# A sum placed between two sets of subtractions, and the last stores with their queues exchanged

## The chip, the cores and the metric

The kernel runs on one core of a Trainium2 chip. The metric is the device time of one execution in microseconds (us); lower is better. Engines are named as in the profile: PE is TensorE (matmuls), DVE is VectorE, ACT is ScalarE, POOL is GpSimd, SP is SyncE, which issues DMAs here and computes nothing. "ACTq" and "SPq" are the DMA-issuing sides of ScalarE and SyncE.

## The reference

A cross-conditioned mixture of three experts over B = 8 batches of T = 512 tokens with H = 256 features, all in float32:

```python
nx = layer_norm(x)                                   # (8, 512, 256)
weights = softmax(nx @ Wq @ (ctx @ Wk)^T / 16)       # 64 context rows per batch
evidence = weights @ (ctx @ Wv)
combined = concat([nx, evidence, anchor])            # 768 features
probs = softmax(combined @ router_W + router_b)      # 3 experts
h = silu(combined @ e_w1 + e_b1)                     # (8, 512, 3, 512)
routed = sum over experts of probs * (h @ e_w2 + e_b2)
g = sigmoid(silu(combined @ gate_w1 + gate_b1) @ gate_w2 + gate_b2)
return x + g * (routed @ out_w + out_b)
```

## The kernel before

The work is a loop of four passes (`j` from 0 to 3), each over two batches, called rows 0 and 1. Before the loop weights are loaded, products of weights are formed (`e_w2 @ out_w`, for instance, becomes `w2o`), and the first two batches are normalized. A pass runs `gate_layer`, three times `expert_layer`, and `outputs`. Everything is kept transposed: features on the 128 partitions, the 512 tokens along the free axis. A float32 product of 128x128 weights with 512 columns shows in the profile as two MATMUL rows of PE.

The products of 2x2 blocks (two feature halves by two batches) are computed with seven block products in place of eight, in the manner of Strassen and Winograd: sums and differences of weight blocks are prepared once (`w2s`, picked by `combo(S1)`, `combo(S2)`, `combo(S4)`), and differences of the hidden tiles are formed by VectorE in `subtract` (line 1072), which overwrites one block of the hidden tiles with the difference of two. One call of `subtract` issues three instructions, one for each expert, each over 128x1024 elements. `experts(ps, lhs, k, i)` issues the six products (twelve MATMUL rows, line 796) that contract one block of hidden tiles, over all experts, into one bank of TensorE's accumulators. The banks are called `u`, `z` and `y` in `outputs`. A bank goes on accumulating from one block product to the next: the intermediate value is added to a result tile (`r11`, `r12`, `r21`, `r22`) by VectorE and the next products are added on top. That sum is `keep` (line 1088), one VectorE instruction over 128x512 elements which reads the bank and adds it to the result tile.

So around the change the order in `outputs` is: products into `u`, `keep(r11, u)`, products into `z`, two calls of `subtract`, `keep(r22, z)`, products into `u` with `combo(S2)`, `keep(r12, u)`. The second products into `u` read the block that the first `subtract` writes. The block that the second `subtract` writes is read two or more product groups later. In passes 0 to 2 there follow products into `y` and again into `u`, with parts of the next pass between them (`run(...)`), before `z` is used again with `combo(S4)`. In the last pass `z` is used right after.

The program order on each engine is the order in which the code issues its instructions (`manual_schedule`); waits between engines are set from the tiles that they share. Each engine works its instructions off in that order, so an instruction that waits holds up those behind it.

At the end of the last pass things differ from the other passes. Row 0's lower half of features is finished token by token: the tokens are taken as the partition axis, in four tiles of 128 tokens (`token_experts`, six products of 128x128 for each tile, into banks 2, 0, 5 and 3). `turn_rest` transposes the gate and the partial result on TensorE and ScalarE copies them into `rest`. `finish_late` finishes row 0's upper half and stores it as four pieces of `hg`, two on ScalarE's queue and two on SyncE's. Then `finish_rows` (lines 1177 to 1180) runs for each of the four token tiles: a product and a sum on VectorE, and one store of 64 KB from `y_rows`. The stores of tiles 0 and 2 go to SyncE's queue and those of tiles 1 and 3 to ScalarE's. A DMA issue on any of these queues also waits until an earlier DMA that has the same completion semaphore has landed; eight such semaphores are used in turn by the DMAs of both queues.

Of the kernel before, what the change touches and what calls it, by code (L numbers as in the profile page):

```python
# [16 lines left out]
def kernel(  # L17
# [51 lines left out]
    nc = tc.nc  # L69
# [28 lines left out]
    def bank(i, name):  # L98
        return psum.tile([P, 512], F32, tag=f"b{i}", name=name)
# [908 lines left out]
    def outputs(j, steps):  # L1008
        last = j == NP - 1

        def run(point):
            for step in steps.get(point, ()):
                step()
# [17 lines left out]
        u, z, y = (bank(i, f"ps_g{n}_{j}") for n, i in (("u", 0), ("z", 2), ("y", 4)))  # L1031
# [25 lines left out]
        def experts(ps, lhs, k, i, start=False):  # L1057
            for q in range(NQ):
                product(ps, lhs(q), hidden(j, q, k, i), start=start and q == 0)

        def combo(s):
            return lambda q: w2s[:, s, q, :]

        def subtract(dst, other):

            (k, i), (k2, i2), (k3, i3) = dst, *other
            for e in range(E):
                d, p, m = (
                    S["h", ii, e].rearrange("p (q k) t -> p q k t", k=2)[:, :, kk, :]
                    for kk, ii in ((k, i), (k2, i2), (k3, i3))  # L1070
                )
                nc.vector.tensor_tensor(d, p, m, ALU.subtract)  # L1072

        def bias_sum(role, i, row):

            r = work.tile([P, T], F32, tag=role, name=f"{role}_{j}", bufs=1)
            nc.scalar.activation(
                by_side(r), pb[:, row, :, 1, :], AF.Identity, bias=b2o[:, i, 0:1],
                scale=b2o[:, i, 1:2],
            )  # L1080
            for e in range(2, E):
                nc.vector.scalar_tensor_tensor(  # L1082
                    by_side(r), pb[:, row, :, e, :], b2o[:, i, e : e + 1], by_side(r), ALU.mult, ALU.add
                )
            return r

        def keep(r, ps):
            nc.vector.tensor_tensor(r, r, ps, ALU.add)  # L1088
# [32 lines left out]
        def finish_late(r, ps, i, row):  # L1121
# [5 lines left out]
        r11, r22, r12, r21 = (  # L1127
            bias_sum(f"r{i + 1}{row + 1}", i, row) for i, row in ((0, 0), (1, 1), (0, 1), (1, 0))
        )
        ug = u  # L1130
        u, y, z = (bank(i, f"ps_{n}2_{j}") for i, n in ((1, "u"), (3, "y"), (5, "z")))
# [4 lines left out]
        run("P1")  # L1136
        experts(z, combo(S1), 0, 1, start=True)
        subtract((0, 1), ((1, 1), (0, 1)))
        subtract((0, 0), ((0, 1), (0, 0)))
        keep(r22, z)  # L1140
        run("P5")
        experts(u, combo(S2), 0, 1)
        keep(r12, u)
# [17 lines left out]
        def turn_rest(r):  # L1161

            rest = work.tile([P, 2, NT, P], F32, tag="xg", name="rest", bufs=1)
            for n, part in enumerate((S["hg", 0, 0], r)):
                pt = misc(f"pt_rest_{n}")
                for t in range(NT):
                    ts = slice(t * P, (t + 1) * P)
                    nc.tensor.transpose(pt[:, ts], part[:, ts], ident)
                nc.scalar.copy(rest[:, n, :, :].rearrange("p t c -> p (t c)"), pt)
            return rest  # L1170
# [6 lines left out]
        def finish_rows(y, rest, ps, t, queue):  # L1177
            nc.vector.tensor_tensor(y, ps, rest[:, 0, t, :], ALU.mult)
            nc.vector.tensor_tensor(y, y, rest[:, 1, t, :], ALU.add)
            queue.dma_start(out[2 * j, t * P : (t + 1) * P, :P], y)  # L1180
# [8 lines left out]
        rest = turn_rest(r11)  # L1189
        experts(u, lambda q: a(q, 1, 1), 0, 1)  # L1190
        tokens = [bank(b, f"ps_tokens_{b}")[:, :P] for b in (2, 0, 5, 3)]
# [2 lines left out]
        finish_late(r21, u, 1, 0)  # L1194
        y = work.tile([P, NT, P], F32, tag="yb", name="y_rows")
        for t in range(NT):
            finish_rows(y[:, t, :], rest, tokens[t], t, nc.scalar if t % 2 else nc.sync)


    with tc.manual_schedule(engines=None):  # L1200
# [62 lines left out]
        for j in range(NP):  # L1263
# [80 lines left out]
            for e in range(E):  # L1344
                expert_layer(j, e, within)
            outputs(j, between)


# [32 lines left out]
```

## Time and profile before

| | |
|---|---|
| median of 3 runs | 462.98 us (462.89 to 463.24) |
| profiled execution, device time | 463.12 us |
| its span (first to last event shown) | 461.3 us |
| mean granted TensorE clock | 0.999 |
| PE busy | 456.4 us (99%) |
| DVE busy | 365.2 us (79%) |
| ACT busy | 214.7 us (47%) |
| POOL busy | 100.4 us (22%) |

The span is what the profile covers; the execution's own time is 1.8 us longer and is what the runs are compared by. Times in the text are microseconds from the start of the span unless they are durations. In lists of instructions the first number is the start, the second the length, then engine, line, operation, output <- inputs, and in brackets how long the engine had been idle and what ended it. TensorE's matmuls overlap, so the length of a row is longer than the distance to the next one; distances between starts are the better measure.

### The profile page before, as it was taken

Reading aid. Unit: us, or ns where it says so; the run is one execution under the profiler, and the core shown is the slowest. Engines: PE = TensorE matmul, PEld = TensorE weight load, DVE = VectorE, ACT = ScalarE, POOL = GpSimd, SP = SyncE. Lnnn points to the kernel's source line nnn. Section 1 sums busy time; section 2 is a strip of 40 time slices with the busy share of each in tenths; the row PEclk is TensorE's granted clock in tenths of the full one; section 3 lists DMA queues with packets and bytes.
Section 4 is the critical chain, followed back from the end, with each engine's and each line's share of the span. In section 5 each row is a group of like instructions: output and inputs, shape, how many; then the busy total and the mean of one; then the engine's idle time right before and its main releaser. Section 6 shows DMA issues by size and latency. Waiting matters only on the chain.

```text
span 461.3 us, 4752 instructions
## 1 busy us (share of the span) xinstructions
PE 456.4 (99%) x1455; PEld 210.1 (46%) x1455; DVE 365.2 (79%) x683; ACT 214.7 (47%) x370; POOL 100.4 (22%) x149
## 2 busy tenths in 40 slices
PE   9999999999999999999999999999999999999996
PEld 7544555444444444444444444444444444444445
DVE  2988979969799669869799659879889625787973
ACT  3445683664222666556221576548221456457000
POOL 6357715001181200001072300001072300000020
PEclk9999999999999999999999999999999999999999
DMA  8975677302013326802012235702011570000013
GB/s 275 370 158 128 102 232 126 83 0 46 7 23 46 76 87 142 159 18 46 6 24 32 37 136 120 110 0 46 6 24 23 82 195 0 0 0 1 0 22 70
DMA packets 119401, 35.27 MB, mean 76 GB/s; under 512 B 106044, under 2 KB 116336, under 8 KB 118864
## 3 DMA queue, kind: packets, MB, share of 16 engines
q1 hardware_dynamic: 115312, 27.02, 28.9%
q0 software_dynamic: 2176, 7.17, 4.7%
q10 hardware_dynamic: 1888, 0.79, 0.6%
q8 instruction: 11, 0.18, 0.2%
q14 instruction: 14, 0.11, 0.1%
HBM read 27.56 MB, written 7.39 MB: 76 GB/s over the span
## 4 chain that ended last, share of the span: by engine, by line
PE 95%; DVE 4%; issue 0%
PE ps_u L796 43%; PE ps_z L796 18%; PE ps_y L796 14%; PE ps_vw L771 5%; PE ps_gu L796 3%; PE ps_w2o L501 2%; PE ps_s L649 2%; PE ps_gz L796 1%; DVE h L1072 1%; PE ps_tokens L796 1%; PE ps_wake L294 1%; DVE h L880 1%; PE ps_v L339 1%; PE ps_m L339 1%; PE ps_gy L796 1%; DVE r L1082 0%
## 5 line engine op out<-in xcount | busy, mean ns | idle before, releaser
L880 DVE TENSOR_TENSOR h<-h,pb 128x512 f32<-128x512 f32 x96 | 61.9, 694 | 6.5 <-ACT h L829 6.5
L796 PE MATMUL ps_u<-h,w2o 128*128 128x512 f32 x144 | 64.2, 595 | 0.0
L829 ACT ACTIVATE h<-h,abias 128x512 f32<-128x512 f32 x72 | 49.6, 719 | 13.5 <-DVE h L835 13.0
L796 PE MATMUL ps_u<-nxT,w 128*128 128x512 f32 x112 | 55.3, 604 | 0.0
L796 PE MATMUL ps_z<-wT,vw 64*128 64x512 f32 x104 | 49.5, 605 | 0.0
L1105 POOL TENSOR_TENSOR yb<-yb,xb 128x512 f32<-128x512 f32 x14 | 17.8, 1269 | 142.9 <-DVE yb L1104 138.8
L796 PE MATMUL ps_z<-h,w2s 128*128 128x512 f32 x96 | 42.6, 593 | 0.2 <-DVE r L1088 0.2
L796 PEld LDWEIGHTS ps_u<-h,w2o 128*128 128x128 f32 x144 | 27.0, 190 | 32.7 <-issue 29.4
L838 ACT COPY h<-ps_u 128x512 f32<-128x512 f32 x48 | 28.0, 582 | 29.4 <-PE ps_u L796 26.9
L415 POOL DMA_DIRECT2D vrd<-vw x8 | 5.0, 630 | 136.9 <-ACT vw L778 136.9
L1072 DVE TENSOR_TENSOR h<-h,h 128x1024 f32<-128x1024 f32 x24 | 34.3, 1483 | 0.0
L796 PEld LDWEIGHTS ps_u<-nxT,w 128*128 128x128 f32 x112 | 20.2, 189 | 29.5 <-issue 24.2
L829 ACT ACTIVATE h<-ps_u,abias 128x512 f32<-128x512 f32 x24 | 16.5, 688 | 29.7 <-PE ps_z L796 29.4
L796 PEld LDWEIGHTS ps_z<-h,w2s 128*128 128x128 f32 x96 | 18.1, 190 | 23.5 <-issue 21.8
L796 PE MATMUL ps_y<-nxT,w 128*128 128x512 f32 x56 | 28.6, 592 | 0.0
L796 PE MATMUL ps_z<-T,ws 128*128 128x512 f32 x56 | 28.6, 592 | 0.0
L835 DVE TENSOR_TENSOR h<-h,ps_y 128x512 f32<-128x512 f32 x24 | 16.4, 683 | 14.8 <-PE ps_y L796 14.0
L796 PE MATMUL ps_u<-wT,vw 64*128 64x512 f32 x56 | 27.8, 611 | 0.0
L796 PE MATMUL ps_y<-wT,vw 64*128 64x512 f32 x56 | 27.0, 596 | 0.0
L771 PE MATMUL ps_vw<-w,vT 128*128 128x512 f32 (+1 forms) x64 | 26.9, 542 | 0.0
L796 PE MATMUL ps_u<-T,ws 128*128 128x512 f32 x56 | 26.6, 592 | 0.0
L796 PE MATMUL ps_u<-T,w 128*128 128x512 f32 x56 | 26.6, 592 | 0.0
(229 smaller groups left out, 792.2 us busy)
## 6 DMA issues: line engine op xcount, KB each, us to landing
pb<-pd POOLq DMA_DIRECT2D x4, 1536.0 KB, 6.5
xb<-in_x_dram SPq DMA_DIRECT2D x64, 64.0 KB, 2.4
out_dram<-yb SPq DMA_DIRECT2D x56, 64.0 KB, 2.0
w<-in_L_xcond_e_w_dram SPq DMA_DIRECT2D x6, 512.0 KB, 10.1
x<-in_x_dram SPq DMA_DIRECT2D x24, 128.0 KB, 2.9
xd<-x SPq DMA_DIRECT2D x24, 128.0 KB, 2.4
xg<-xd SPq DMA_DIRECT2D x48, 64.0 KB, 2.4
scr_wa<-in_L_xcond_e_w_dram SPq DMA_DIRECT2D x3, 512.0 KB, 16.5
```

What stands on the lines that cost most here:

```text
L339: nc.tensor.matmul(ps, w_sb[:, k, m * P : (m + 1) * P], src[:, k, :], start=(k == 0), stop=(k == KH - 1))
L415: nc.gpsimd.dma_start(S["vrd", j][i].rearrange("e c -> c e"), S["vw", j][row_half(i), R0:])
L501: nc.tensor.matmul(ps[:, d * H : (d + 1) * H], w2T[:, k, (i + d) * P : (i + d + 1) * P], ow_sb[:, k, :], start=(k == 0), stop=(k == KH - 1),)
L649: nc.tensor.matmul(ps[side(i, h), g * NH : (g + 1) * NH], mr[:, k, 2 * j + i, g * TB : (g + 1) * TB], S["nxT", 2 * j + i][:, k, h * NH : ( ...
L771: nc.tensor.matmul(ps, vT[:, k, j * 2 * CT : (j + 1) * 2 * CT], w1[:, KH + k, n0:n1], start=(k == 0), stop=(k == KH - 1),)
L796: nc.tensor.matmul(ps, lhsT, rhs, start=start, stop=True, skip_group_check=not start)
L829: nc.scalar.activation(h, h if src is None else src, AF.Silu, bias=abias[:, c, 2 * j + i : 2 * j + i + 1])
L835: nc.vector.tensor_tensor(h, h, part, ALU.add)
L838: nc.scalar.copy(chunk(n, i, d), part)
L880: nc.vector.tensor_tensor(h, h, S["pb", j][:, i, :, 2 * q // RC, :], ALU.mult)
L1072: nc.vector.tensor_tensor(d, p, m, ALU.subtract)
L1105: nc.gpsimd.tensor_tensor(yb, yb, S["xb", 2 * j + row][:, i, :], ALU.add)
```

## The change

It has two parts. In `outputs`, in all four passes, VectorE's sum `keep(r22, z)` is issued between the two calls of `subtract` instead of after the second. In the last pass, the four stores of `y_rows` have their queues exchanged: tiles 0 and 2 are issued from ScalarE's queue and tiles 1 and 3 from SyncE's. No instruction is added or removed.

```diff
         run("P1")
         experts(z, combo(S1), 0, 1, start=True)
         subtract((0, 1), ((1, 1), (0, 1)))
+        keep(r22, z)
         subtract((0, 0), ((0, 1), (0, 0)))
-        keep(r22, z)
         run("P5")
         experts(u, combo(S2), 0, 1)
         keep(r12, u)
...
         finish_late(r21, u, 1, 0)
         y = work.tile([P, NT, P], F32, tag="yb", name="y_rows")
         for t in range(NT):
-            finish_rows(y[:, t, :], rest, tokens[t], t, nc.scalar if t % 2 else nc.sync)
+            finish_rows(y[:, t, :], rest, tokens[t], t, nc.sync if t % 2 else nc.scalar)
```

## The prediction

> **What bounds the kernel now.** I read the page first, for the span and for what each engine waits on; then the chain of waits over the last pass, because both edits can only count where that chain passes; then the timeline around the two places.
>
> The page:
>
> ```profile
> span 461.3 us, 4752 instructions
> PE 456.4 (99%) x1455; PEld 210.1 (46%) x1455; DVE 365.2 (79%) x683; ACT 214.7 (47%) x370; POOL 100.4 (22%) x149
> L796 PE MATMUL ps_z<-h,w2s 128*128 128x512 f32 x96 | 42.6, 593 | 0.2 <-DVE r L1088 0.2
> ```
>
> TensorE is busy 456.4 of 461.3 us, so only two things can shorten the run: fewer gaps between matmuls, or a shorter head or tail where no matmul runs. The third line shows a gap that belongs to the change: of the 96 matmuls into the bank `z` (four passes of 24), the whole group waited 0.2 us in the run, and VectorE's sums of L1088 (`keep`) ended that wait.
>
> The chain of waits, last pass (start, length, what):
>
> ```profile
> 427.43 0.60 DVE r L1088
> 428.03 6.81 DVE h L1072 x6
> 434.84 0.61 DVE r L1088
> 435.45 0.04 issue
> 435.49 5.42 PE ps_z L796 x12
> 440.91 5.15 PE ps_u L796 x12
> 446.06 0.87 PE pt_rest L1168 x8
> 446.93 5.32 PE ps_u L796 x12
> 452.25 5.37 PE ps_tokens L796 x48
> ```
>
> Up to 435.45 the end of the run hangs on VectorE: a sum, six subtractions, another sum. From 435.49 on it hangs on TensorE until the tokens. The DVE line at 434.84 is `keep(r22, z)`, the instruction that the change moves. The timeline there, with the two neighbouring matmul groups:
>
> ```profile
> 429.98 5.31 PE L796 MATMUL ps_u<-h,w2s 128*128 128x512 f32 x12
> 431.35 3.49 DVE L1072 TENSOR_TENSOR h<-h,h 128x1024 f32<-128x1024 f32 x3
> 434.76 0.68 DVE L1088 TENSOR_TENSOR r<-r,ps_z 128x512 f32<-128x512 f32 x1
> 435.36 0.68 DVE L1088 TENSOR_TENSOR r<-r,ps_u 128x512 f32<-128x512 f32 x1
> 435.49 5.42 PE L796 MATMUL ps_z<-h,w2s 128*128 128x512 f32 x12 [0.20 <-DVE r L1088]
> 440.75 5.31 PE L796 MATMUL ps_u<-h,w2o 128*128 128x512 f32 x12
> ```
>
> The group at 435.49 accumulates on into `z`, so it must not start before `keep(r22, z)` has read the bank. That read ends at 435.44.
>
> The tail: the timeline, then SyncE's own waits (line, what it waited for, us in total, times, longest), then the DMA issues (us from issue to landing last).
>
> ```profile
> 457.98 0.29 DVE L1179 TENSOR_TENSOR y_rows<-y_rows,rest 128x128 f32<-128x128 f32 x1
> 458.30 0.36 ACTq L1180 DMA_DIRECT2D out_dram<-y_rows  x1
> ```
>
> ```profile
> SPq L1376 <- DMA out_dram<-y_rows: 2.1, 1, 2.1
> SPq L1180 <- DMA out_dram<-hg: 1.6, 1, 1.6
> ```
>
> ```profile
> out_dram<-y_rows ACTq DMA_DIRECT2D x1, 64.0 KB, 1.7
> ```
>
> Tile 3's store leaves on ScalarE's queue 0.03 us after its sum, lands 1.7 us later at 460.0, and the end of the program follows at 461.3. Note the second wait: tile 0's store, on SyncE's queue, was ready at 455.03 but was issued at 456.99, because it first waited for an earlier `hg` store to land. With tile 0 that wait hides.
>
> **The change part by part.**
>
> *Sum moved ahead of the second subtractions, passes 1 to 3.* No instruction is added or removed; on VectorE one sum moves past three subtractions, in each of four passes. It can only hurt if `z` is not complete at the new place. In pass 2 the matmuls into `z` end at 219.23 and the new place is 220.75; in pass 4 it is 430.14 against 431.35. The margin is 1.2 to 1.5 us, and it is built in: the third subtraction of the first set overwrites tiles that the last matmuls into `z` read, so it starts after those anyway. The second subtractions come one sum (0.60 us start to start, 434.76 to 435.36) later, and what follows them comes at the old time. Their result is read first by matmuls starting at 231.33 in pass 2 (it would be written by 220.75 + 0.60 + 3.49 = 224.84) and at 440.75 in pass 4 (by 435.44): covers of 6.5 and 5.3 us, 4.8 if those matmuls move up. No DMA moves with it, and GpSimd's queue is not passed. In passes 1 to 3 the next matmuls into `z` come only after two other groups, and the page's 0.2 us of wait is all used by pass 4. Cost and gain there: 0.
>
> *The same in pass 4.* The next matmuls into `z` follow at once. With the sum at 431.35 it ends near 432.03, and TensorE, whose previous group still runs, no longer waits. How much is that? The annotated idle is 0.20 us. But by starts, 429.98 to 440.75 is 10.77 us for two groups of twelve; where nothing waits, such a group takes 5.15 us (219.07 to 224.22 in pass 2), two take 10.30. The stall is 0.47 us: 0.36 up to the start of the group, since its weights too were loaded only after the sum, and 0.11 in its first matmuls, refilling. The Trainium skill, "TensorE: Matmul & The Clock Gate", Part 2, "Step-by-step: what each phase is for", says that back-to-back matmuls hide the drain of one behind the fill of the next, and that only an isolated one pays it; it puts the drain at about 128 cycles at 2.4 GHz, 53 ns. By that rule the break would be worth about 0.20 + 0.05 = 0.25 us (an estimate from that page); by the rows 0.47. The starts are measured and include the late weight load, so I take 0.47 and keep 0.2 as the lower end.
>
> *What is late next.* VectorE frees up for `keep(r12, u)` at 435.36 as before, so its following work keeps its old times: three more subtractions, both early finishes, `r12` done at 445.35. Is that early enough? The next read of `u` (L1102 for `r22`) starts at 446.10 after 0.74 us of idle; moved up by 0.47 it starts at 445.63, still 0.27 after VectorE is free. The last group into `u` waits for that read, so it moves up too. ScalarE's copies of `rest` and GpSimd's additions follow the same starts. From 452.29 on VectorE waits on TensorE, and the token sums follow the matmuls. So the shift reaches the last sum, which ends at 457.80 instead of 458.27. Gain on the path: 0.47.
>
> *Queues exchanged.* Tiles 0 and 2 go from SyncE to ScalarE, tiles 1 and 3 the other way; the same four stores, two on each queue. ScalarE has no compute left after its `rest` copies, done by 447.6, so nothing is queued behind its stores. Tile 0, now behind ScalarE's two `hg` stores (ending at 455.42, moved up to 454.95), leaves near 455.0. Tile 1 takes tile 0's place on SyncE, and its wait for the `hg` store: issued at 454.49 - 0.47 = 454.02, plus the same 2.45, gives 456.5. Its own issue takes 0.38, so SyncE is free at 456.9, and tile 3, ready at 457.80, has 0.9 us in hand. On that queue the two `y_rows` stores landed after 1.6 us, tile 3 on the other after 1.7: -0.1 us. The spread of all four (1.6 to 2.5, the long one issued amid the `hg` stores) bounds the unknown effect at -0.1 and +0.9; I take -0.05, by the nearest rows, those issued in a nearly empty queue. A rule speaks against the exchange: the Trainium skill, "Perfetto Trace Analysis", "Per-engine timelines", says that hardware-generated stores share one descriptor generator under a lock, so one issue can wait for another. Tile 1 and tile 2 would now be issued almost together (456.5 and 456.46 + 0.03), where tiles 0 and 2 went in series on one queue. By the rows an issue is 0.36 to 0.55 us; if one must wait for the whole of the other that is at most 0.55, and it lies inside tile 3's 0.9. Both ways the sum is the same unless the hand is used up.
>
> *Sum.* 0.47 + 0.05 = 0.52 us less. The profiled execution took 463.12 us, 1.8 more than its span, and is 0.14 above the median of 462.98. Carried to the median: 462.46, call it 462.5, or -0.11%. A change of about 0.2% (0.93 us) is what a measurement of this kernel can tell from none, so this counts as no change.
>
> **The rivals.**
>
> *The gap closes and reopens.* Something I see as just in time (the 0.27 us of VectorE before the read of `u`) runs late, and the end moves by 0.2 us or not at all: 462.8 to 463.0. For it: VectorE is on the chain right up to 435.45, and its work after that doesn't move. Against: the 0.74 us of idle. Chance 0.2; also "no change".
>
> *More than the gap.* The exchange pays as well, e.g. if SyncE, which waits for the last store (2.1 us), closes sooner on a store of its own. Bound: the shortest landing of 1.6 against 1.7 gives 0.1, and of the 1.3 us from landing to end I know no part that the queue decides. To reach 0.93 it would have to give 0.46. At 1.0 us: 462.0. Chance 0.1.
>
> *Slower, by one mechanism: tile 3 stuck behind tile 1 on SyncE.* Before, the tile behind the `hg` wait was followed by tile 2; now it is followed by the last tile of the kernel. It costs one for one once the `hg` store takes more than 2.45 + 0.9 = 3.35 us to land. The longest landing in this tail is 3.0. Earlier traffic speaks for it: tile 0 now joins at 455.0 while the DMA engines already carry the `hg` stores. To be slower than before the landing must pass 3.9, and for 0.2% slower 4.8; at 5.0 the time is 462.98 - 0.52 + 1.65 = 464.1. Chance 0.06.
>
> **How the numbers follow.** Forecast 0.64, reopened gap 0.2, more than the gap 0.1, stuck store 0.06. Predicted time 462.5, the likeliest case. The forecast's own range is 462.3 to 462.8 (0.47 or 0.2, and the 0.1 of landing). The range wanted takes in the reopened gap, with the 0.35 us that the three runs of before spread over, and the edge of the larger gain: 462.0 to 463.2. Faster by over 0.2%: most of the third case, 0.09. Slower: 0.06. Within: 0.85.
>
> **What would show it.** Right, in the profile after: the sum on `ps_z` near 431.35 and ahead of three subtractions; the matmuls into `z` of the last pass starting near 435.13 with no idle from L1088; the next group near 440.28; `r22`'s read of `u` near 445.6 with about 0.3 us of idle; the tokens ending near 457.1; SyncE issuing tile 1 near 456.5 and tile 3 near 457.8. Wrong: a wait on VectorE ahead of the moved sum; TensorE idle elsewhere after 435; tile 3 issued well after its sum; or a landing of the last store that is not 1.6 to 1.7.

## The result and the profile after

| | before | changed |
|---|---|---|
| median | 462.97 us (462.75 to 463.49, 22 runs) | 462.30 us (462.15 to 462.70, 22 runs) |
| profiled execution | 463.12 us | 462.29 us |
| its span | 461.3 us | 460.5 us |

The ratio is 0.9984, 95% interval 0.9979 to 0.9990. The medians are 0.67 us apart, where 0.52 us was forecast: the change is small, inside the 0.2% band, but it is not nothing. The interval leaves out 1, and every run of the changed kernel lies below every run of before, so less than the 0.2% of the prediction can be told from no change here.

The page, the three lines that were shown of before:

```profile
span 460.5 us, 4752 instructions
PE 456.0 (99%) x1455; PEld 210.2 (46%) x1455; DVE 365.3 (79%) x683; ACT 214.7 (47%) x370; POOL 100.3 (22%) x149
L796 PE MATMUL ps_z<-h,w2s 128*128 128x512 f32 x96 | 42.5, 592 | 0.0
```

Instruction counts are those of before, and no busy time differs by more than 0.4 us. What is gone is the last column of the third line, the 0.2 us that matmuls into `z` waited for VectorE.

The chain of waits, last pass:

```profile
430.07 5.15 PE ps_u L796 x12
435.22 5.15 PE ps_z L796 x12
440.37 5.15 PE ps_u L796 x12
445.52 0.88 PE pt_rest L1168 x8
446.40 5.32 PE ps_u L796 x12
451.72 5.37 PE ps_tokens L796 x48
...
457.12 0.30 DVE y_rows L1178
457.44 0.29 DVE y_rows L1179
```

VectorE's stretch of sums and subtractions is off the chain. The groups into `u`, `z` and `u` stand exactly 5.15 us apart; before, the one into `z` took 5.42 on the chain and came after a wait. (The chain counts a group from the end of the row ahead of it, 0.16 us later than its start in the timeline; the distances are the same.)

The timeline there:

```profile
429.91 5.31 PE L796 MATMUL ps_u<-h,w2s 128*128 128x512 f32 x12
431.27 0.68 DVE L1088 TENSOR_TENSOR r<-r,ps_z 128x512 f32<-128x512 f32 x1
431.87 3.49 DVE L1072 TENSOR_TENSOR h<-h,h 128x1024 f32<-128x1024 f32 x3
435.06 5.31 PE L796 MATMUL ps_z<-h,w2s 128*128 128x512 f32 x12
435.28 0.68 DVE L1088 TENSOR_TENSOR r<-r,ps_u 128x512 f32<-128x512 f32 x1
440.21 5.31 PE L796 MATMUL ps_u<-h,w2o 128*128 128x512 f32 x12
445.56 0.69 DVE L1102 TENSOR_TENSOR r<-r,ps_u 128x512 f32<-128x512 f32 x1 [0.29 <-PE ps_u L796]
```

The sum stands at 431.27 with no wait ahead of it. From the start of the group into `u` to that of the next one into `u` it is now 440.21 - 429.91 = 10.30 us, where it was 10.77: 0.47 us. VectorE still idles 0.29 us before it reads `u` (the bracket in the last line), so nothing took the gap's place.

The tail: timeline, then SyncE's own waits.

```profile
457.44 0.29 DVE L1179 TENSOR_TENSOR y_rows<-y_rows,rest 128x128 f32<-128x128 f32 x1
457.76 0.36 SPq L1180 DMA_DIRECT2D out_dram<-y_rows  x1
```

```profile
SPq L1180 <- DMA out_dram<-hg: 1.6, 1, 1.6
SPq L1376 <- DMA out_dram<-y_rows: 0.9, 2, 0.8
SPq L1180 <- DVE y_rows L1179: 0.9, 1, 0.9
```

Tile 3's store is issued 0.03 us after its sum. SyncE had waited 0.9 us for that sum by then: tile 1, ahead of it, was held by the `hg` store for the same 1.6 us that tile 0 was before, and was gone in time. From the last sum (457.73) to the end of the span (460.49) the tail is 2.76 us, where it was 3.08 (461.35 - 458.27).

So the profiled spans differ by 0.86 us: 0.47 in the gap, 0.32 in the tail, and 0.07 that was there ahead of the last pass's gap (429.98 against 429.91; in the profiles of the experiments it is anywhere from 429.89 to 430.33). The tail has more in it than the forecast's 0.05. SyncE's end-of-program list accounts for most of it. The code ends with a list of waits on SyncE, one for each of the eight completion semaphores that the last stores use, in a fixed order, before the engines meet. Each wait is a row of its own, and in before they stand 0.06 us apart (460.03, 460.09, and so on to 460.45). The rows of SyncE's waits from the last landing to the meeting of the engines, of before and then of the changed kernel (count, ns each, first and last start):

```profile
L1376 SPq EVENT_SEMAPHORE  x8: 28/28/28, 460.0 to 460.5; - x8
```

```profile
L1376 SPq EVENT_SEMAPHORE  x4: 28/28/28, 459.4 to 459.6; - x4
```

Before, tile 3's store carried the first semaphore of the list: SyncE stood at it until the landing, and then had seven more rows to pass, though all of those stores had long landed. With the queues exchanged tile 3's store carries the fifth. The first four are passed while it is in flight, and three remain behind it. Four rows of 0.06 us are 0.24 us. The rest, 0.07, is the landing itself: 1.73 us from issue to the passing of the wait before, 1.66 after. That part is scatter: in the next experiment the store is ScalarE's, as in before, and the same stretch took 1.65.

### The profile page after: what moved, and what is told of

Read it like the earlier page. It is cut to its first block, busy times and chain, and to the rows that moved or that the text cites. A ratio compares the mean times of both kernels' runs of the same rounds, so it can differ in the third digit from the quotient of the medians.

```text
span 460.5 us, 4752 instructions
## 1 busy us (share of the span) xinstructions
PE 456.0 (99%) x1455; PEld 210.2 (46%) x1455; DVE 365.3 (79%) x683; ACT 214.7 (47%) x370; POOL 100.3 (22%) x149
## 4 chain that ended last, share of the span: by engine, by line
PE 99%; DVE 0%; issue 0%
PE ps_u L796 45%; PE ps_z L796 20%; PE ps_y L796 14%; PE ps_vw L771 5%; PE ps_gu L796 3%; PE ps_w2o L501 2%; PE ps_s L649 2%; PE ps_gz L796 1%; PE ps_tokens L796 1%; PE ps_wake L294 1%; PE ps_v L339 1%; PE ps_m L339 1%; PE ps_gy L796 1%; PE pt_x L579 0%; PE pt_ctx L318 0%; PE ps_ar L440 0%
```

## The experiments

Each is measured beside before on the same chip. Before's median was 463.00 us beside the two parts alone, tile 3 alone on ScalarE's queue and tile 3 alone on SyncE's; 463.09 beside the sum moved later, the sum moved in three passes and all four stores on ScalarE's queue; and 463.02 beside the last two. So a median is good to about 0.1 us from one of these sets to another.

**The two parts alone.** The sum moved, the queues as before:

```diff
         subtract((0, 1), ((1, 1), (0, 1)))
+        keep(r22, z)
         subtract((0, 0), ((0, 1), (0, 0)))
-        keep(r22, z)
```

> The sum moved between the subtractions, queues of the last stores as before. Theory A (the gap in TensorE's stream is 0.47 us, and the rest of the 0.67 us between the medians comes from the tail): 0.47 us less than before, 462.5; in the profile the last pass's matmuls into z start 5.15 us after the group ahead of them and the tail from the last VectorE sum to the end of the span stays at about 3.0 us. Rival B (the move alone is worth all of it, the queues nothing): 0.67 less, 462.3, with a tail of about 2.8 us.

Measured: 462.53 us, ratio 0.9990 (0.9982 to 0.9998), 0.47 less than before. The timeline of this kernel:

```profile
429.94 5.31 PE L796 MATMUL ps_u<-h,w2s 128*128 128x512 f32 x12
431.30 0.68 DVE L1088 TENSOR_TENSOR r<-r,ps_z 128x512 f32<-128x512 f32 x1
435.09 5.31 PE L796 MATMUL ps_z<-h,w2s 128*128 128x512 f32 x12
```

The group into `z` starts 5.15 us after the one ahead, and the tail is 3.00 us with seven rows behind the landing, 0.24 more than in the changed kernel with three. Theory A holds, rival B falls.

The queues alone:

```diff
-            finish_rows(y[:, t, :], rest, tokens[t], t, nc.scalar if t % 2 else nc.sync)
+            finish_rows(y[:, t, :], rest, tokens[t], t, nc.sync if t % 2 else nc.scalar)
```

> The sum where it was before, only the queues of the last four stores exchanged. Theory A: TensorE's gap of 0.47 us stays, the tail gets 0.2 to 0.3 us shorter: 462.7 to 462.8. Rival B: no change, 463.0.

Measured: 462.81 us, 0.19 less; ratio 0.9996 (0.9987 to 1.0004), which by itself can't be told from no change. The profile tells it apart: the gap stays, and the tail is 2.69 us.

```profile
430.33 5.31 PE L796 MATMUL ps_u<-h,w2s 128*128 128x512 f32 x12
435.84 5.42 PE L796 MATMUL ps_z<-h,w2s 128*128 128x512 f32 x12 [0.19 <-DVE r L1088]
```

The group into `z` starts 5.51 us after the one ahead. This execution was 0.35 us late ahead of the gap (430.33 against 429.98), at a place that the exchange can't reach, so a single span, 461.3 us as in before, doesn't show the gain. The two parts add up: 0.47 + 0.19 = 0.66, against 0.67 for both, which is closer than the medians are known.

**The move in other doses.** The sum later than before:

```diff
         subtract((0, 0), ((0, 1), (0, 0)))
-        keep(r22, z)
         run("P5")
         experts(u, combo(S2), 0, 1)
         keep(r12, u)
+        keep(r22, z)
```

> The opposite of the change: keep(r22, z) one sum later than before, behind keep(r12, u), in all four passes; queues as before. Theory A (in the last pass TensorE waits for this sum, one for one): the sum starts at about 435.96 in place of 434.76 and its bank is free about 1.2 us later; TensorE's group into z starts 1.2 us later than before, at about 436.7, and the next group the same, so about 1.2 us more than before, 464.2. Rival E (the gap of before was the bank's and matmul pipeline's own, not the wait for the sum): no change, 463.0. In the first three passes no matmul waits for it by either.

Measured: 464.07 us, 0.98 more; ratio 1.0022 (1.0013 to 1.0031). The timeline:

```profile
429.92 5.31 PE L796 MATMUL ps_u<-h,w2s 128*128 128x512 f32 x12
435.27 0.69 DVE L1088 TENSOR_TENSOR r<-r,ps_u 128x512 f32<-128x512 f32 x1 [0.49 <-PE ps_u L796]
435.88 0.68 DVE L1088 TENSOR_TENSOR r<-r,ps_z 128x512 f32<-128x512 f32 x1
436.61 5.42 PE L796 MATMUL ps_z<-h,w2s 128*128 128x512 f32 x12 [1.38 <-DVE r L1088]
441.87 5.31 PE L796 MATMUL ps_u<-h,w2o 128*128 128x512 f32 x12
```

From `u` to `u` it is now 11.95 us, 1.18 more than before: the matmuls wait for this sum one for one, and rival E falls. The idle in brackets grew by the same 1.18 (0.20 to 1.38), so the stall is the idle plus a constant 0.27. The single rows of TensorE show where the 0.27 lies, alike in both kernels. A row is 0.592 us long, but where nothing waits the next one starts 0.429 after it; the idle in brackets counts from the end of the row, which leaves out 0.163. And the weights of the first matmul into `z` are loaded at its own start (435.49 and 436.61) instead of about 0.43 ahead of it, as in the changed kernel (434.63 for the row at 435.06); that first row takes 0.697, 0.105 longer.

The end moved by less than 1.18, by 0.98 between the medians. One row of the list fewer stands behind the landing (six), which is 0.06. In the profiled execution the landing was also shorter (1.59 us in place of 1.73), which makes its tail 2.87; whether that holds for the medians is not shown.

The sum moved in the first three passes only:

```diff
+        if not last:
+            keep(r22, z)
         subtract((0, 0), ((0, 1), (0, 0)))
-        keep(r22, z)
+        if last:
+            keep(r22, z)
```

> The sum moved as in the change in passes 1 to 3 only; in the last pass and for the queues as before. Theory A: all of the gain of the move is in the last pass, so no change from before, 463.0 within 0.1. Rival F (a part of the 0.47 us comes from the earlier passes, 0.1 us or more from each): 462.7 or less.

Measured: 463.04 us, ratio 1.0000 (0.9991 to 1.0008). The gap of the last pass is as before:

```profile
429.98 5.31 PE L796 MATMUL ps_u<-h,w2s 128*128 128x512 f32 x12
...
435.49 5.42 PE L796 MATMUL ps_z<-h,w2s 128*128 128x512 f32 x12 [0.20 <-DVE r L1088]
```

At 429.98, where before has it too, nothing of three moved sums has reached TensorE. The interval alone reaches to 0.4 us, but rival F asked for 462.7 or less, and the fastest of the 13 runs is 462.86. Rival F falls.

**What sets the tail.** Three ways of sharing out the stores, with the sum moved in each. A store's semaphore does not go by its queue alone: with the sum moved later, all stores on the queues of before, tile 3's store got the second place in the list in place of the first. Nor are the eight taken strictly in turn: in before two stores 4.7 us apart, with three stores between them, have the same one. The rule was not looked for; each store's place is read from its trace. So the place in the list can be varied without SyncE's queue being the last one's. First, tile 3 alone on ScalarE's queue:

```diff
-            finish_rows(y[:, t, :], rest, tokens[t], t, nc.scalar if t % 2 else nc.sync)
+            finish_rows(y[:, t, :], rest, tokens[t], t, nc.scalar if t == 3 else nc.sync)
```

> The sum moved; the stores of tiles 0 to 2 on SyncE's queue, only tile 3's on ScalarE's. By this the completion semaphore of tile 3's store becomes the last of eight in SyncE's list of waits at the end of the program (it was the first of the eight before, and the fifth in the changed kernel). Theory C (the tail depends on how many waits of that list still come after the last landing, about 0.06 us each): seven fewer than before, 0.42 us, with the gap 0.89 less than before, 462.1, and faster than the changed kernel. Rival D (the tail got shorter because SyncE closes sooner on a store of its own queue): the tail of before, 3.0 us, and 0.47 less than before, 462.5.

Measured: 462.07 us, 0.93 less than before; ratio 0.9981 (0.9973 to 0.9988). SyncE's rows from the last landing to the meeting:

```profile
L1376 SPq EVENT_SEMAPHORE  x1: 28/28/28, 459.5 to 459.5; - x1
```

One row, the one that ended with the landing; none behind it. The tail is 2.52 us, though the store is ScalarE's, as in before. Rival D, which gave 3.0, falls.

Second, tile 3 alone on SyncE's queue, with everything else of the tail on ScalarE's:

```diff
-            store(g, i, row, slice(0, T), (nc.scalar, nc.sync))
+            store(g, i, row, slice(0, T), (nc.scalar,))
...
-            finish_rows(y[:, t, :], rest, tokens[t], t, nc.scalar if t % 2 else nc.sync)
+            finish_rows(y[:, t, :], rest, tokens[t], t, nc.sync if t == 3 else nc.scalar)
```

> The sum moved; tile 3's store alone on SyncE's queue, and the four hg stores and tiles 0 to 2 on ScalarE's. Tile 3's semaphore is then the first of the eight in SyncE's list at the end, as before, but its store is SyncE's own. Theory C: the seven waits come after the landing again, tail about 2.9 to 3.0 us, 462.4 to 462.5. Rival D: the short tail of the changed kernel, 2.77 us, and 462.3. If the hg stores, now all in one queue, landed after tile 3's store, the tail would be longer than 3.0.

Measured: 462.81 us, ratio 0.9995 (0.9987 to 1.0003). The same rows:

```profile
L1376 SPq EVENT_SEMAPHORE  x8: 28/28/28, 459.7 to 460.1; - x8
```

Eight rows and a tail of 2.92 us although the store is SyncE's own: by the tail theory C holds. The median is a miss: 0.3 to 0.5 us over what the two theories gave. About 0.2 us of it lies outside the span. The execution is longer than its span by 1.88 to 2.02 us in each of this kernel's 13 runs, mean 1.97; in every run of before and of the kernels above it is 1.72 to 1.84, mean 1.78. The spans themselves are 0.41 us shorter than before's in the mean, and theory C, with all of before's rows, asked for 0.47.

Third, all four token stores on ScalarE's queue:

```diff
-            finish_rows(y[:, t, :], rest, tokens[t], t, nc.scalar if t % 2 else nc.sync)
+            finish_rows(y[:, t, :], rest, tokens[t], t, nc.scalar)
```

> The sum moved; all four token stores on ScalarE's queue. Tile 3's semaphore is then the fourth of the eight in SyncE's list at the end (first before, eighth with tile 3 alone on ScalarE's queue), on the same queue as in both. Theory C (about 0.07 us for each wait behind it): four waits instead of seven behind it, tail from the last sum to the end of the span 2.8 us, 462.3. Rival D (the queue sets the tail): the tail of before, 3.05 us, 462.5. Rival G (it is SyncE's having no late store of its own, as with tile 3 alone): the tail of 2.5 us or less, 462.1.

Measured: 462.64 us, ratio 0.9991 (0.9983 to 0.9999). The rows:

```profile
L1376 SPq EVENT_SEMAPHORE  x5: 28/28/28, 459.3 to 459.6; - x5
```

Four rows behind the landing, tail 2.74 us: between seven rows (3.00 us with the sum moved) and none (2.52) on the same queue. Rivals D and G fall. The median again is 0.3 us over what theory C gave. Again more lies outside the span, 1.93 to 2.04 us in all 13 runs, mean 1.99. The spans are 0.64 us shorter than before's in the mean; the gap and three rows make 0.65. Taken from 463.09 that is 462.44; the forecast of 462.3 had a row at 0.07 and before at 463.0. So inside the span both kernels do what theory C says. They have seven and six of the last eight stores on ScalarE's queue, the others at most four. What the 0.2 us outside the span are was not found and no run takes them apart; it stays open.

The tails above hold the landing as well, and that scatters: the changed kernel, profiled twice, has tails of 2.76 and 2.86, tile 3 alone on ScalarE's queue 2.52 and 2.68. From the passing of the last store's wait to the end of the span there is no landing any more. All eleven profiled executions, sorted by the rows behind that wait:

| rows behind | kernels | queue of the last store | passing to end of span, us |
|---|---|---|---|
| 7 | before; sum moved only; in three passes only | ScalarE | 1.318, 1.321, 1.313 |
| 7 | tile 3 alone on SyncE's queue | SyncE | 1.314 |
| 6 | sum later | ScalarE | 1.256 |
| 4 | all four on ScalarE's queue | ScalarE | 1.132 |
| 3 | changed, twice; queues only | SyncE | 1.074, 1.067, 1.073 |
| 0 | tile 3 alone on ScalarE's queue, twice | ScalarE | 0.895, 0.894 |

It is 0.89 us and 0.06 more for each row, whichever queue the store is on.

**The version with the lowest median, beside the changed kernel.** Both once more on one chip:

> The changed kernel once more, so that it and the version with tile 3 alone on ScalarE's queue run on one chip. 462.3; three waits after the last landing.

> The sum moved, tiles 0 to 2 on SyncE's queue and tile 3 on ScalarE's, beside the changed kernel. Theory C: three waits of 0.06 us fewer behind the last landing than the changed kernel, 0.2 us less than it, 462.1. If the 462.07 of its first runs was chance: 462.3, the same as the changed kernel.

Measured: 462.35 us for the changed kernel (ratio 0.9983, 0.9976 to 0.9989) and 462.16 us with tile 3 alone on ScalarE's queue (0.9981, 0.9973 to 0.9988), 0.19 us apart; in the first runs it was 462.30 and 462.07. Three rows of 0.06 us are 0.18. The intervals against before overlap widely, so the order of the two rests on two pairs of medians that agree, and on the count of rows (three and none behind the landing, as before).

## Why the prediction was right, point by point

That the time stayed inside the 0.2% band says little for the argument: any gain from nothing to 0.9 us would have done the same. What speaks for it is that the profile's signs came as they were named, each within 0.1 us. The time itself, 462.30, lies at the fast edge of the forecast's own 462.3 to 462.8, because of the one term that was wrong.

- *The gap in the last pass, 0.47 us.* Right: 10.77 to 10.30 us between starts in the profile, and 0.47 between medians with the move alone. That the medians agree to the hundredth is luck. The choice between the row and the rule is settled as well. The Trainium skill's "TensorE: Matmul & The Clock Gate", Part 2, "Step-by-step: what each phase is for", puts the drain at about 128 cycles; with the annotated idle that made an estimate of 0.25 us. The break cost 0.47, and in the larger dose the same 0.27 came on top of the idle. Here the measured starts decide.
- *Nothing in the first three passes.* Right: 463.04 against 463.09 with the move there alone.
- *No new wait.* Right: 0.29 us of VectorE idle before the read of `u` where 0.27 was worked out, so the gap did not reopen. That rival is out.
- *Tile 3 stuck behind tile 1.* It did not happen. SyncE's time in hand behind the `hg` wait was worked out as 0.9 us, and SyncE idled 0.9 us before tile 3. The `hg` store landed in the same time as before with tile 0 earlier beside it.
- *One issue waiting for another.* Tile 1 and tile 2 were issued at 456.44 and 456.43, and each issue took 0.36 to 0.37 us, no longer than a lone one. No lock wait is seen in this one pair, and the sum did not depend on it.
- *The exchange, -0.05 us.* This term was mis-sized: 0.19 us by the medians, 0.24 by four rows of the list, 0.32 in the profiled tail with the scatter of the landing. The prediction looked at where the landing times of the two queues differ (1.6 and 1.7 us, bound 0.1) and said of the 1.3 us from landing to end "I know no part that the queue decides". That is the step that failed, and the forecast held in spite of it only because the part is small. The queue doesn't decide it, but which semaphore the last store carries does, and exchanging the queues moved that from the first place in SyncE's list to the fifth. It was to be seen: before's SyncE has seven rows after 460.03 that are waits for stores landed by 459.01.
- *The rival "more than the gap".* It named the right place, SyncE's closing, for a wrong reason (a store of its own) and with a price of 0.46 us or more; the real size, a quarter of a microsecond, left the result within 0.2%.

## What to carry to other kernels

When an accumulating bank is read in the middle and then written again, look for which matmul group comes next on that bank, and put the read ahead of any VectorE work that this group doesn't need; size the stall by the distance between starts of the groups around it, since the idle in brackets was 0.27 us short of it here, at an idle of 0.20 us as at one of 1.38. At the end of a kernel, look also at what the closing engine still does after the last landing. Here it is a list of waits passed in a fixed order, and a last store whose semaphore stands late in that list is worth up to seven rows of 0.06 us.

## What was not expected of the hardware

A wait on SyncE for a semaphore that had long been reached still took 0.06 us of its sequence in every kernel looked at, with a row of 28 ns. The two queues themselves made no difference to the last store: the time from its issue to the passing of its wait was 1.57 to 1.75 us on ScalarE's queue (seven executions) and 1.58 to 1.77 on SyncE's (four). And about 0.2 us more lay outside the span in the two kernels with most of the last stores on ScalarE's queue, for which no cause was found.
